# Three re-orderings in a two-layer image kernel: when a weight is loaded, when accumulators are seeded, when weight sums are made

## The chip, the cores and the metric

The kernel runs on one core of one Trainium2 chip. Its five engines work side by side, each through its own queue of instructions in order: PE (TensorE, matrix products; its weight loads are shown apart as PEld), DVE (VectorE), ACT (ScalarE), POOL (GpSimd) and SP (SyncE, which here only issues transfers). Sixteen DMA engines move data between the chip's memory, where the arrays lie, and the on-chip memory SBUF. PE writes into PSUM, eight banks from which DVE and ACT read. The metric is the device time of one execution in microseconds, the median over several runs.

## What is computed

Two layers over an image batch of 2 x 56 x 56 positions with 384 channels, in float32. The first layer is neighbourhood attention and an MLP. The second, around which the change lies, is this (cut to what matters):

```python
h = layernorm(x, n1_g, n1_b)
p = h @ w_in + b_in                                  # 384 -> 768
local = depthwise_conv_3x3(p, k_conv)
lr, rl = ema(local, axis=2), ema(local, axis=2, reverse=True)
tb, bt = ema(local, axis=1), ema(local, axis=1, reverse=True)
mixed = layernorm(0.25 * (lr + rl + tb + bt) + local, on_g, on_b)
x = x + (mixed @ w_out + b_out)                      # 768 -> 384
h2 = layernorm(x, n2_g, n2_b)
x = x + (gelu(h2 @ w1 + b1, approximate=False) @ w2 + b2)   # 384 -> 1536 -> 384
```

with `ema` the recurrence y[i] = 0.6 y[i-1] + 0.4 x[i].

## The kernel before

The 6272 positions are 49 tiles of 128 rows, taken in groups of four (one group has a single tile). The function `passes` holds everything after the attention.

The first pass goes over the groups of the first layer's MLP and, a group behind, the second layer's first normalisation and the product with `w_in` (`project_in`). Its result goes to the chip's memory (`p_d`).

The convolution and the four recurrences run on DVE and ACT beside PE's products. A small planner (`Beside`) holds a list of jobs: a `Band` loads some rows of one 128-channel slice (`pt`, L1280), multiplies by the centre tap on ACT (`loc`, L1295), adds the eight other taps on DVE (L1312), scans the lines both ways (`both`, L1258 and L1262), stores to `loc_d` and `mix_d` (L1320), and has POOL add `both` into `mix_d` (L1331). A `Columns` job does the vertical scans: loads (`loc`, L1350), turns (`line`, L1360), scans, turns back (`mixed`, L1378), and adds to `mix_d` through POOL. `beside.go(us)` is called after each block of PE's work and emits as many steps of these jobs as fit in the time given. This is a budget used when the program is written out; on the chip each engine follows its own order. The pool `conv` holds these tiles, with two buffers for loads, three for `loc` and `line`, four for `both` and `mixed`.

The second pass begins after the last `project_in`. Its weights `w1` and `w2` of the second layer come from `weights(1)` in three parts each (`w_parts`, 768 KB a part, L674, on SP's queue). The parts of `w1` are issued in the first pass's last group, the parts of `w2` right behind the last `project_in`.

The first three groups of the second pass (`dgroups[:switch]`, groups 0 to 2) run beside the convolution. A group does:
- twelve hidden blocks (m = 0 to 11): three matmuls of 128x512 (the profile shows each as two) into one of three PSUM banks `mm` (L1205), then gelu on ACT (L1216) into `hid`. Between them, statistics of the next group's `mixed` tokens: six transposing matmuls (`xi`, L1448), then DVE (L221, L222). Behind block 6, POOL turns these into a standard deviation `sd` and its inverse `rs` (L229, L230);
- `project_out` for the next group: six products with `w_out` (twelve matmuls as profiled) for each of four tiles. Tiles 0, 1 and 3 accumulate onto a bank, `y` or `y_end`, that ACT has seeded with the residual times `sd` (`seed_out`, L1487); ACT multiplies the result by `rs` (L1498). Tile 2 is evicted by DVE (L1508). The first two seeds of the group are written ahead, before the last hidden block;
- four products with `w2` (L1223, `y<-w,hid`), onto banks seeded by ACT (L1233), evicted by ACT (L2040).

From group 3 on (the tail), the two MLP products are made by a scheme of seven products in place of eight (`hidden_by_seven`, `tokens_by_seven`), which needs sums and differences of quarters of the weights and inputs: `w1_sums`, `xsums`, and four sums of `w2` (`sums_of_w2`, L1715, DVE). The sums of `w2` are needed in `tokens_by_seven`. In `hidden_by_seven`, three rounds u = 0, 1, 2 each make matmuls into `ua`, `uz` and `ub` (L1657); ACT copies `ub` out in between (L1690, L1696, L1703); DVE adds (`hid_u`: L1704, and L1676 within `finish`); gelu is L1664; POOL makes three sums of hidden blocks (L1721 to L1723). Twice in a round the loop calls `next(measuring)`, which emits one step of measuring the next group's tokens on DVE: a step is eight transposes of 32x192 (L1460); every second step also has statistics. Then `project_out` makes four tiles with DVE evicting each (L1508). Its hook `then(k)` issues, for k = 0, the last `finish`; before the change also one sum of `w2` per tile, in the first tail group alone; and the measuring of the fourth tile.

The tail's tiles come from a pool `tail` opened where `conv` has been closed, so its tiles lie over those of `conv`, one after the other in the order in which they are first asked for; an instruction that writes such a tile first waits for the last user of what lay there.

Of the kernel before, what the change touches and what calls it, by code (L numbers as in the profile page):

```python
# [45 lines left out]
HID, NHID = 4 * C, 4 * C // P  # L46
# [132 lines left out]
def block_kernel(ctx: ExitStack, tc: tile.TileContext, ins: dict, out: bass.AP):  # L179
    nc = tc.nc  # L180
# [187 lines left out]
    hT = ep.tile([P, NC, PAIR], F32, name="hT")  # L368
# [294 lines left out]
    def weights(layer):  # L663

        w1 = wm.tile([P, NC, HID], F32, name=f"w1_{layer}", tag="w1")
        w2 = wm.tile([P, NHID, C], F32, name=f"w2_{layer}", tag="w2")
        s1 = ins[f"L{layer}_conv_w1"].rearrange("(c p) n -> p c n", p=P)
        s2 = ins[f"L{layer}_conv_w2"].rearrange("(c p) n -> p c n", p=P)
        parts = []
        for h in range(0, HID, HID // 3):  # L670
            parts.append((w1[:, :, h : h + HID // 3], s1[:, :, h : h + HID // 3]))
        for c in range(0, NHID, NHID // 3):
            parts.append((w2[:, c : c + NHID // 3, :], s2[:, c : c + NHID // 3, :]))
        return w1, w2, [lambda q=nc.sync, d=d, s=s: q.dma_start(out=d, in_=s) for d, s in parts]  # L674
# [96 lines left out]
    for q in range(0, len(stream), CHUNKS):  # L771
        part = []
# [92 lines left out]
    for t in range(NS + 2):  # L865
        part = parts[t] if t < NS else []
# [16 lines left out]
        for s in fresh:  # L883
            if s % UG == 0:
                dense = Dense(s // UG)
            if s == NU - UG - 4:
# [3 lines left out]
                w1, w2, w_parts = weights(0)  # L890
# [211 lines left out]
    def passes(xs, xn, w1, w2, between=lambda ps: None):  # L1102
# [9 lines left out]
        switch = 3  # L1112
# [341 lines left out]
        def measure_by_vector(mx, norm, k):  # L1454


            t = tp.tile([P, NI * P], F32, name="turned", bufs=2)
            for i in range(0, P, HD):
                for j in range(0, P, HD):
                    nc.vector.transpose(  # L1460
                        t[j : j + HD].rearrange("p (m c) -> p m c", m=NI)[:, :, i : i + HD],
                        mx[i : i + HD, :, k * P + j : k * P + j + HD],
                    )
                if i == HD:
                    yield
            norm.add(k, [t[:, h * C : (h + 1) * C] for h in range(2)])
            yield
# [63 lines left out]
        sum_steps, seeds = [], []  # L1531
# [72 lines left out]
        def measure_by_steps(ahead, tiles):  # L1604
            for k in tiles:
                yield from measure_by_vector(ahead[0], ahead[2], k)
# [100 lines left out]
        def sums_of_w2(w2, engine=nc.gpsimd):  # L1707

            q = NHID // 2
            b11, b12 = w2[:, :q, : C // 2], w2[:, :q, C // 2 :]  # L1710
            b21, b22 = w2[:, q:, : C // 2], w2[:, q:, C // 2 :]
            t1, t2, t3, t4 = (tp.tile([P, q, C // 2], F32, name=f"w2_t{i}") for i in range(4))
            steps = []
            for to, x, y in ((t1, b12, b11), (t2, b22, t1), (t3, b22, b12), (t4, b21, t2)):
                steps.append(lambda to=to, x=x, y=y: engine.tensor_tensor(to, x, y, ALU.subtract))  # L1715
            return (t1, t2, t3, t4), steps
# [96 lines left out]
        w1_sums = more_of_w1(w1, sums_of_w1(w1, tp.tile([P, NC, HID // 2], F32, name="w1_t")))  # L1813
        x = xs.pop(0)
        hT = channels(xn, groups[0][1], "L0_conv_ln2_g", "L0_conv_ln2_b")
        add_row(x, groups[0][1], "b2_0")

        for g, (t0, n) in enumerate(groups):
# [19 lines left out]
            if g == last:  # L1838
                beside.until((0, NI - 1))
                load_row(0, "b2_1")  # L1840
                ahead = load_mix(0)
                beside.rate = 1.0
            if g < last:
                x_next, n_next = xs.pop(g + 1), groups[g + 1][1]
# [92 lines left out]
            if g == last:  # L1937
                ahead[2].close_both_ways(dgroups[0][1])
                w1, w2_1, w_parts = weights(1)
                for part in w_parts[:3]:  # L1940
                    part()
            if early:
                hT = io.tile([P, NC, MT], F32, name="hT")
            elif 0 < g < last:
                hT = channels(xn_next, n_next, *ln2)
            x2 = io.tile([P, NT, C], F32, name="xc")
            norm = Norm(sm)
            if early:
                for i, _ in enumerate(tokens_by_seven(low, high, *s12, w2, w2_sums, x, x2)):
                    if 0 <= i < n_next:  # L1950
                        turned(xn_next, i, hT)
                    if i == 5:
                        scaled(hT, n_next, *ln2)
                        xsums = sums_of_input(hT)
# [19 lines left out]
            if g == 0:  # L1974
                hT = channels(xn_next, n_next, *ln2)
                xsums = sums_of_input(hT)
                w2_sums, sum_steps = sums_of_w2(w2)
# [11 lines left out]
        g, x2, norm_w = waiting  # L1989
# [6 lines left out]
        hT = channels(xn, groups[g][1], *n1)  # L1996
# [6 lines left out]
        ahead = load_mix(1)  # L2003
        w2 = w2_1
        project_in(g, hT, first_input)
        for part in w_parts[3:]:
            part()
        n2 = "L1_conv_n2_g", "L1_conv_n2_b"

        hT = channels(first["xn"], dgroups[0][1], *n2)  # L2010
        add_row(x3, dgroups[0][1], "b2_1")
        for g, (t0, n) in enumerate(dgroups[:switch]):
            hid = []
            if g == 1:
                three = sums_of_w1(
                    w1, wp.tile([P, NC, INNER], F32, name="w1_t", tag="w_in")
                )
            for m in range(NHID):
                if m == NHID - 1:
                    seeds = [seed_out(*ahead[1:], k) for k in range(2)]  # L2020
                hid.append(hidden(w1, m, hT, n, "L1_conv_b1"))
                beside.go(MLP, measure_beside(m, g + 1, ahead))
            res = x3
            x3, norm, seeds = project_out(
                g + 1, *ahead, seeds=seeds, behind=lambda k: seeded(res, k)
            )
            ahead = load_mix(g + 2)
            for k in range(n):
                if k == n - 1:
                    hT = channels(xn, dgroups[g + 1][1], *n2)  # L2030
                ps = tokens(hid, w2, k, onto=seeds.pop(0))
                if k == 0:
                    norm.shift(dgroups[g + 1][1])
                if k == n - 3:
                    xn = normalized(norm, x3, dgroups[g + 1][1])
                beside.go(ROW)
                if k == n - 1:
                    add_row(x3, dgroups[g + 1][1], "b2_1")
                o = res[:, k, :]
                nc.scalar.copy(o, ps)  # L2040
                nc.sync.dma_start(out=yout[t0 + k * P : t0 + (k + 1) * P, :], in_=o)
                if k + 2 < n:
                    seeds.append(seeded(res, k + 2))
                if g == switch - 1 and k == 2:
                    beside.until((1, NI - 1))
                    cctx.close()
                    tp = pctx.enter_context(tc.tile_pool(name="tail", bufs=1, reuse_waits="tile"))
                    w1_sums = more_of_w1(w1, three, nc.vector)
# [2 lines left out]
        ps_y, ps_u, bank_b, banks_b = open_banks(pctx, "tail")  # L2051
        ps_m = ps_u
        xsums = sums_of_input(hT, nc.vector)
        w2_sums, sum_steps = sums_of_w2(w2, nc.vector)
        for g, (t0, n) in enumerate(dgroups):
            if g < switch:
                continue
            if g == dlast:
                hid = [hidden(w1, m, hT, n, "L1_conv_b1") for m in range(NHID)]
                for k in range(n):  # L2060
                    ps = tokens(hid, w2, k, y_end)
                nc.vector.tensor_copy(rows[:, 1, :], x3[:, n - 1, :])
                assert n == 1 and t0 + n * P == T2
                break
            n_next = dgroups[g + 1][1]
            add_row(ahead[1], n_next, "b_out")
            s1, s2 = (tp.tile([P, NHID // 2, MT // 2], F32, name=x) for x in ("s1", "s2"))
            low, high, finish = hidden_by_seven(
                hT, xsums, w1, w1_sums, (s1, s2), measure_by_steps(ahead, range(min(n_next, 3))),
                "L1_conv_b1",  # L2070
            )
            ahead[2].close(min(n_next, 3))
            more = measure_by_steps(ahead, range(3, n_next))

            def then(k):
                if k == 0:
                    finish()
                if sum_steps:
                    sum_steps.pop(0)()
                next(more, None)  # L2080
                if k == 1 and n_next > 3:
                    ahead[2].close(n_next, first=3)

            res = x3
            x3, norm = project_out(g + 1, *ahead, then)
            if g + 2 <= dlast:
                ahead = load_mix(g + 2)
            hT = io.tile([P, NC, MT], F32, name="hT")
            for i, _ in enumerate(tokens_by_seven(low, high, s1, s2, w2, w2_sums, res, res)):
                if i == 0:  # L2090
                    norm.shift(n_next)
                    xn = normalized(norm, x3, n_next)
                if 1 <= i <= n_next:
                    turned(xn, i - 1, hT)
                if i == 5:
                    scaled(hT, n_next, *n2)
                    xsums = sums_of_input(hT) if n_next == NT else None
                    add_row(x3, n_next, "b2_1")
            nc.sync.dma_start(
                out=yout[t0 : t0 + NT * P, :].rearrange("(k p) c -> p k c", p=P), in_=res  # L2100
            )
# [8 lines left out]
    with tc.If(again > 0):  # L2110
        attention_again()
        w1, w2, w_parts = weights(0)
# [81 lines left out]
```

## Time and profile before

| what | value |
|---|---|
| median of 3 runs | 2573.22 us (2570.5 to 2573.25) |
| profiled execution, own time | 2575.16 us |
| its span, first to last instruction | 2573.4 us |
| mean granted TensorE clock | 0.995 |
| last `project_in`, its p_d store issued | 1654.00 us |
| groups 0, 1, 2 of the second pass, first hidden matmul | 1654.69, 1743.36, 1827.58 us |
| tail, first matmul of `hidden_by_seven` | 1915.46 us |
| first and second `tokens_by_seven` | 1964.41, 2037.59 us |

Times in the trace count from the span's first instruction. A line of a timeline gives the start, the duration, the engine (PEld, and SPq for what SP issues), the line of the program, the operation, its output and inputs, how many instructions were merged, and in brackets the idle time before it with what ended it. A line of waits gives the engine and line that waited, what released it, and the total, the number and the longest. "Granted clock" is the share of full speed at which PE was allowed to run.

### The profile page before, as it was taken

The page shows a single profiled execution, that of the slowest core. Times are in us where ns is not written, and L with a number is a line of the kernel's source. Part 1 is how long each engine was busy: PE and PEld are TensorE (multiplying, and loading weights), DVE is VectorE, ACT ScalarE, POOL GpSimd, SP SyncE. Part 2 cuts the span into 40 slices and gives each one's busy share as a digit, 9 for nine tenths or more (in the row PEclk, how much of TensorE's full clock was granted, in tenths as well). Part 3 has the DMA queues.
Part 4 walks back from the last instruction along what each step waited for, and adds up shares of the span by engine and source line. Part 5 has one row for each costly group of instructions (what it writes and reads, how often), then busy time and mean ns, then how long its engine had stood idle before and what let it go on. Part 6 is the DMA issues. An engine that isn't in the chain of part 4 may idle for free. (4 is left out here: it accounts for less than half of the span.)

```text
span 2573.4 us, 41871 instructions
## 1 busy us (share of the span) xinstructions
PE 2535.8 (99%) x16678; PEld 1736.1 (67%) x16678; DVE 1982.8 (77%) x3706; ACT 1137.3 (44%) x2058; POOL 575.4 (22%) x618
## 2 busy tenths in 40 slices
PE   9999999999999999999999999999999999999999
PEld 5666666666698887455545555555468888888888
DVE  3888878887554453899989999789978877878871
ACT  5655555654443444334455443433862233233222
POOL 0111111111442331010110002112113333333332
PEclk9999999999999999999999999999999999999999
DMA  7423454225522223467677667766780333333210
GB/s 226 150 94 95 148 187 159 86 84 194 158 60 85 68 68 90 140 177 214 177 209 280 209 186 218 232 184 168 207 218 18 74 74 74 74 74 74 47 28 21
DMA packets 155597, 342.97 MB, mean 133 GB/s; under 512 B 11158, under 2 KB 112000, under 8 KB 153088
## 3 DMA queue, kind: packets, MB, share of 16 engines
q1 hardware_dynamic: 124096, 255.65, 29.4%
q0 software_dynamic: 26352, 57.81, 13.2%
q10 hardware_dynamic: 4944, 26.74, 3.0%
q8 instruction: 133, 2.18, 0.4%
q14 instruction: 72, 0.59, 0.1%
HBM read 176.39 MB, written 134.88 MB: 121 GB/s over the span
## 5 line engine op out<-in xcount | busy, mean ns | idle before, releaser
L1312 DVE SCALAR_TENSOR_TENSOR loc<-pt,taps,loc 128x495 f32<-128x495 f32 (+13 forms) x288 | 372.7, 1294 | 38.2 <-ACT loc L1295 29.5
L1205 PE MATMUL mm<-hT,w 128*128 128x512 f32 x720 | 318.9, 597 | 4.4 <-ACT hid L1216 4.2
L581 ACT ACTIVATE pts<-pts 119x448 f32<-119x448 f32 (+5 forms) x396 | 210.7, 573 | 109.4 <-DVE pts L571 100.3
L571 DVE TENSOR_TENSOR pts<-sc,bias 119x448 f32<-119x448 f32 (+5 forms) x396 | 219.2, 616 | 45.2 <-PE sc L560 44.9
L1205 PEld LDWEIGHTS mm<-hT,w 128*128 128x128 f32 x720 | 135.2, 191 | 166.4 <-issue 155.4
L1188 DVE STREAM_TRANSPOSE hT<-xn 32x96 f32<-32x96 f32 x784 | 211.2, 269 | 26.7 <-ACT xn L265 16.6
L414 PE MATMUL ps<-hT,wqkv 128*128 128x448 f32 x504 | 206.5, 554 | 2.1 <-ACT vs L459 1.5
L1460 DVE STREAM_TRANSPOSE turned<-mx 32x192 f32<-32x192 f32 x528 | 194.8, 369 | 10.2 <-DMA mix_d<-mixed 3.4
L1223 PE MATMUL y<-w,hid 128*128 128x384 f32 x552 | 181.9, 486 | 0.0
L1223 PE MATMUL y_end<-w,hid 128*128 128x384 f32 x552 | 181.8, 486 | 0.0
L1223 PEld LDWEIGHTS y_end<-w,hid 128*128 128x128 f32 x552 | 104.6, 190 | 72.1
L1223 PEld LDWEIGHTS y<-w,hid 128*128 128x128 f32 x552 | 104.3, 190 | 71.3 <-issue 0.5
L1216 ACT ACTIVATE hid<-mm,chan 128x512 f32<-128x512 f32 x120 | 82.1, 685 | 156.7 <-PE mm L1205 156.7
L414 PEld LDWEIGHTS ps<-hT,wqkv 128*128 128x128 f32 x504 | 91.9, 191 | 85.5 <-issue 75.4
L1205 PE MATMUL mm<-hT,w_in 128*128 128x512 f32 x324 | 140.8, 593 | 0.6 <-DVE hid_u L1676 0.6
L1331 POOL DMA_DIRECT2D mix_d<-both x36 | 31.8, 884 | 417.6 <-ACT both L1327 357.3
L1657 PE MATMUL ua<-hT,w 128*128 128x256 f32 x504 | 122.5, 379 | 0.0
L560 PEld LDWEIGHTS sc<-qT,kT 32*100 32x100 f32 (+3 forms) x3168 | 87.8, 169 | 46.8 <-DVE sum L590 7.6
L600 PE MATMUL o<-pts,vt 100*32 100x112 f32 (+3 forms) x3168 | 116.3, 263 | 0.9 <-ACT pts L581 0.9
L1205 PEld LDWEIGHTS mm<-hT,w_in 128*128 128x128 f32 x324 | 61.2, 190 | 77.5 <-issue 72.2
L1664 ACT ACTIVATE hid<-hid_u,chan 128x256 f32<-128x256 f32 x168 | 76.1, 500 | 82.0 <-DVE hid_u L1676 67.5
L237 POOL TENSOR_TENSOR rs<-rs,mhalf 128x4 f32<-128x4 f32 (+4 forms) x56 | 50.2, 897 | 277.2 <-DVE rs L234 276.1
(217 smaller groups left out, 5007.6 us busy)
## 6 DMA issues: line engine op xcount, KB each, us to landing
loc<-loc_d SPq DMA_DIRECT2D x24, 784.0 KB
xa<-x_d SPq DMA_DIRECT2D x24, 768.0 KB
xa<-rows POOLq DMA_DIRECT2D x24, 768.0 KB, 11.9
bias<-in_bias_t ACTq DMA_DIRECT2D x13, 1344.0 KB
p_d<-mx SPq DMA_DIRECT2D x11, 1536.0 KB
mx<-mix_d SPq DMA_DIRECT2D x11, 1536.0 KB
v_d<-vs SPq DMA_DIRECT2D x49, 192.0 KB
xr<-in_x SPq DMA_DIRECT2D x49, 192.0 KB
```

What stands on the lines that cost most here:

```text
L414: nc.tensor.matmul(ps, lhsT=wqkv[:, c, m * P : (m + 1) * P], rhs=hT[:, c, half_of(n)], start=c == 0, stop=c == NC - 1,)
L560: nc.tensor.matmul(sc[i // 2][: w.keys, i % 2, q : q + TT], lhsT=kT[d, hg, w.keys_at + r * w.kc : w.keys_at + (r + w.rows) * w.kc], rhs=qT ...
L571: nc.vector.tensor_tensor(self.pts[:n, h : h + 2, lo:hi, :], sc[half][:n, :, at * TT : (at + hi - lo) * TT].rearrange("p h (c q) -> p h c ...
L581: nc.scalar.activation(t, t, AF.Exp)
L600: nc.tensor.matmul(o[i * HD : (i + 1) * HD, self.slot, :TT], lhsT=w.vt[:n, c, h * HD : (h + 1) * HD], rhs=self.pts[:n, i, c, :], start=c = ...
L1188: nc.vector.transpose(hT[j : j + HD, :, k * P + i : k * P + i + HD], xn[i : i + HD, k, :].rearrange("p (c q) -> p c q", c=NC)[:, :, j : j ...
L1205: nc.tensor.matmul(ps[:, : n * P], lhsT=w[:, c, m * P : (m + 1) * P], rhs=hT[:, c, : n * P], start=c == 0, stop=c == NC - 1,)
L1216: nc.scalar.activation(t[:, : n * P], ps[:, : n * P], AF.Gelu, bias=col(b1, m))
L1223: nc.tensor.matmul(ps, lhsT=t[:, k * P : (k + 1) * P], rhs=w[:, m, :], start=m == 0 and onto is None, stop=m == len(lhs) - 1, skip_group_c ...
L1312: nc.vector.scalar_tensor_tensor(to, pt[:, lo + dy - self.top : hi + dy - self.top, xt : xt + n], self.tap(dy, dx), to, ALU.mult, ALU.add,)
L1460: nc.vector.transpose(t[j : j + HD].rearrange("p (m c) -> p m c", m=NI)[:, :, i : i + HD], mx[i : i + HD, :, k * P + j : k * P + j + HD],)
L1657: nc.tensor.matmul(bank[:, i, :], lhsT=w[:, m * P : (m + 1) * P], rhs=x, start=start and i == 0, stop=True, skip_group_check=True,)
```

## The change

Three edits in `passes`.

1. The three parts of `w2` (`w_parts[3:]`) are no longer issued right after the last `project_in`. They are issued in group 0 of the second pass, one each ahead of the hidden blocks m = 4, 6 and 8. In the program as built, SP's queue then has two loads of `pt`, one store to `loc_d` and one to `mix_d` ahead of the three parts, where they stood behind them; the three parts stay next to each other.
2. The first two seeds of `w_out`'s accumulators are written ahead of hidden block 10 in place of 11, in each of the three groups. On ACT the two L1487 move past one hidden gelu, in group 0 also past one `loc`, in group 2 also past four `mixed`.
3. The four sums of `w2` on DVE are made in the first tail group's `hidden_by_seven`, one behind each of the measuring steps 2 to 5 (counted from 0), in place of one behind each tile of `project_out`. Their tiles are asked for at step 2, so after `s1`, `s2`, `hid_u1`, `hid_u2` and `turned` and not before them; the tail pool's layout changes with it.

The number of instructions on each engine is the same.

```diff
@@ second pass, ahead of its groups @@
         project_in(g, hT, first_input)
-        for part in w_parts[3:]:
-            part()
         n2 = "L1_conv_n2_g", "L1_conv_n2_b"
@@ groups 0 to 2 @@
             for m in range(NHID):
-                if m == NHID - 1:
+                if g == 0 and m in (4, 6, 8):
+                    w_parts.pop(3)()
+                if m == NHID - 2:
                     seeds = [seed_out(*ahead[1:], k) for k in range(2)]
                 hid.append(hidden(w1, m, hT, n, "L1_conv_b1"))
                 beside.go(MLP, measure_beside(m, g + 1, ahead))
@@ tail @@
         xsums = sums_of_input(hT, nc.vector)
-        w2_sums, sum_steps = sums_of_w2(w2, nc.vector)
+        w2_sums = None
+
+        def with_sums(steps):
+
+            nonlocal w2_sums
+            for i, _ in enumerate(steps):
+                if w2_sums is None and i == 2:
+                    w2_sums, sum_steps = sums_of_w2(w2, nc.vector)
+                if i >= 2 and sum_steps:
+                    sum_steps.pop(0)()
+                yield
+
...
+            steps = measure_by_steps(ahead, range(min(n_next, 3)))
             low, high, finish = hidden_by_seven(
-                hT, xsums, w1, w1_sums, (s1, s2), measure_by_steps(ahead, range(min(n_next, 3))),
+                hT, xsums, w1, w1_sums, (s1, s2), with_sums(steps) if g == switch else steps,
                 "L1_conv_b1",
             )
...
                 if k == 0:
                     finish()
-                if sum_steps:
-                    sum_steps.pop(0)()
                 next(more, None)
```

## The prediction, made before the changed kernel was run

> **What bounds the kernel now.** I read the engines' busy times first, then TensorE's waits, then the timelines around each wait that the change can touch. The first line of the page settles the kind of answer:
>
> ```profile
> PE 2535.8 (99%) x16678; PEld 1736.1 (67%) x16678; DVE 1982.8 (77%) x3706; ACT 1137.3 (44%) x2058; POOL 575.4 (22%) x618
> ```
>
> TensorE (PE) carries the span. The change neither adds nor removes a matmul, so it can only change PE's gaps and the half-speed matmuls behind some of them. PE's waits from 1650 us to the end are five (total, times, longest):
>
> ```profile
> PE mm L1205 <- ACT hid L1216: 4.2, 1, 4.2
> PE y_end L1223 <- ACT y_end L1487: 4.0, 1, 4.0
> PE xi L1448 <- DVE st L221: 2.7, 1, 2.7
> PE y L1749 <- DVE xc L1508: 2.3, 1, 2.3
> PE ub L1657 <- issue: 2.2, 1, 2.2
> ```
>
> PE's timeline gives place and after-effect (start, duration, group, gap before it):
>
> ```profile
> 1669.64 2.74 PE L1205 MATMUL mm<-hT,w 128*128 128x512 f32 x6
> 1676.63 5.49 PE L1205 MATMUL mm<-hT,w 128*128 128x512 f32 x6 [4.25 <-ACT hid L1216]
> ...
> 1865.31 5.83 PE L1223 MATMUL y_end<-w_out,mx 128*128 128x384 f32 x12 [4.04 <-ACT y_end L1487]
> ...
> 1922.27 1.10 PE L1657 MATMUL ub<-xsums,w_t 128*128 128x256 f32 x4 [2.19 <-issue]
> ...
> 1964.41 5.85 PE L1749 MATMUL y<-w,hid 128*128 128x192 f32 x24 [2.25 <-DVE xc L1508]
> ```
>
> Behind three gaps the same matmuls take longer: six take 5.49 instead of 2.74 (and the next transposes 0.92 instead of 0.82), twelve 5.83 instead of 4.03, twenty-four 5.85 instead of 4.06. In half-microsecond windows the granted clock stands at 0.50 there (1675.5 to 1682, 1866.5 to 1869.5, 1965.5 to 1968.5). So the gaps cost 4.25+2.75+0.10 = 7.1, 4.04+1.80 = 5.84, 2.25+1.79 = 4.04 and 2.19 us. The gap before xi (2.72 us, at 1754.95) has no slow matmuls behind it.
>
> **Part 1, w2 later: 7.1 us.** Why ACT was late at 1676 is in its timeline, and SP's tells why the load was:
>
> ```profile
> 1663.38 0.69 ACT L1216 ACTIVATE hid<-mm,chan 128x512 f32<-128x512 f32 x1 [1.89 <-PE mm L1205]
> 1674.78 1.23 ACT L1295 ACTIVATE loc<-pt,taps 128x1120 f32<-128x1120 f32 x1 [10.71 <-DMA pt<-p_d]
> ...
> 1654.00 0.37 SPq L1546 DMA_DIRECT2D p_d<-mx  x1
> 1654.47 5.77 SPq L674 DMA_DIRECT2D w<-in_L_conv_w  x3
> 1663.86 2.19 SPq L1280 DMA_DIRECT2D pt<-p_d  x2
> ```
>
> The band's centre tap L1295 sits fourth in ACT's queue, ahead of the fourth hidden block, and waits for its pt load. That load goes out behind three pieces of w2 (3 x 768 KB) on SP's queue. ACT stands still 10.7 us, PE's three mm banks fill, PE stops at 1672.4. Afterwards the three issues (5.77 us of SP) stand behind pt x2, loc_d and mix_d. What follows them on SP is a pt load at 1689.40, far behind. The reader of w2 (y<-w,hid) starts at 1711.09; the stretch's DMA traffic, the same bytes, has ended by 1681.5 (DMA share 1.0 before, 0.03 after), so about 30 us cover it, and only w2 landing later than that would cost PE, one for one.
>
> pt may not go before p_d is stored: released by 1663.9 as now, or sooner with w2 out of the way. Its landing alone is not shown. Nearest rows are POOL's accumulating stores on another queue: 756 to 784 KB in 6.7 to 10.4 us, 532 KB in 8.1 us, for 588 KB here. At best it lands before ACT asks (1664.1); at worst 8 us after 1663.9, at 1671.9. L1295 (1.23) and one hid (0.69) then end at 1673.8, a 1.4 us gap, so the part is worth 5.7 to 7.1. I take 7.1, as landing by 1670.5 is enough and w2 is no longer ahead. DVE gains up to the 9.82 us that it idled before 1676.04, but the next band's centre (L1295 at 1693.75) stands behind a hid that PE paces, so from there it moves with PE. The xi gap stays.
>
> **Part 2, seeds one hidden block earlier: 5.84 us, less 0.2.** In the third group ACT runs hid, four `mixed`, hid, four `mixed` (the second half held 0.52 us by a DMA), two seeds, hid:
>
> ```profile
> 1861.05 1.66 ACT L1378 ACTIVATE mixed<-line 128x392 f32<-128x392 f32 x2
> 1863.23 1.65 ACT L1378 ACTIVATE mixed<-line 128x392 f32<-128x392 f32 x2 [0.52 <-DMA mix_d<-mixed]
> 1864.68 0.58 ACT L1487 ACTIVATE y_end<-xa,sd 128x384 f32<-128x384 f32 x1
> ```
>
> Moved ahead of hid 10, the seeds stand behind the first four `mixed`, which end at 1860.75. The first is done at 1861.33, when PE's last hidden matmul ends (1861.27): no gap. Hid 10 comes 1.1 us later; its bank has no later user in the loop. The second four `mixed` now delay hid 11 and the first eviction to 1866.2, 0.9 us after PE is done, so ACT and DVE gain some 5.0 where PE gains 5.84. The last seed of this group is written at 1906.46 for a PE that wants it at 1907.12, 0.66 of slack, so about 0.2 comes back. In groups 0 and 1 PE does not wait for the seeds: nothing. They need `sd` from POOL (L230), ready at 1689.4 and 1772.4 against a hid 9 ending at 1691.3 and 1775.6.
>
> **Part 3, w2's sums.** Removed: two L1715 (2.41 and 1.33) ahead of the third w_out eviction. DVE reaches it at 1963.75, 3.74 earlier without them, and y would be free at 1960.6, before PE wants it at 1962.15. All 4.04 us go.
>
> A side effect: the tail pool hands out memory in the order of first request. In the built programs hid_u1's first buffer lies at byte 142240 before, inside the last `mixed` tile (139360 to 145632), whose store DVE's and ACT's first tail instructions then await:
>
> ```profile
> 1921.58 0.59 ACT L1696 COPY hid_u<-ub 128x512 f32<-128x512 f32 x1 [4.43 <-DMA mix_d<-mixed]
> ```
>
> After, it lies at 123808, in a `line` tile that ACT has finished by 1910.55; the sums' own tiles take the `mixed` places, and are written some 5 us after that store has landed. So the 2.19 gap at 1922 goes.
>
> Added: the four sums between measuring steps. In one round of the loop DVE has two eight-block transposes (3.06 each), statistics (1.2), L1676 (0.69) and L1704 (0.64), 8.7 us in PE's 9.5; it idles 0.92 before each L1676. Then ACT needs 1.4 (a gelu pair, L1696) before PE's next ub matmuls, with 0.3 to spare (1931.54 against 1931.84). Before the first L1676 one sum of 1.33 is added: 1.33-0.92-0.30 = 0.1 late. Before the second, three: 3.99-1.84-0.30-0.1 = 1.75 late. The second sum overlaps POOL's last sum of hidden (L1723); together such a pair took 2.41 and 2.38 instead of 1.33 and 1.27, so some 0.25 more. New gaps: 2.1 us in all (bounds: 1.85 uncontended; 3 x 2.41 less the slack and one half-speed stretch of 1.8, 6.9). The fourth sum delays L1704 and the first eviction by about 1.3, absorbed by DVE's 1.96 idle before the third L1676.
>
> Whether the new gap halves the clock: the row at 1964 (2.25 us) says 1.79 more, the rows at 1922 (2.19) and 1754 (2.72) say nothing more; I take nothing, two rows of three. The Trainium skill (TensorE: Matmul & The Clock Gate, section "Why this matters for your kernels") allows idle gaps up to about 3 us before the clock halves; by it the removed gap at 1964 would be worth 2.25, not 4.04, and the sum 1.8 less. The trace disagrees there (0.50 after 2.25 us), and decides.
>
> **Sum.** 7.1+5.84-0.2+4.04+2.19-2.1 = 16.9 us. The profiled execution took 2575.16 for a span of 2573.4; the runs' median is 2573.22. From the median: 2556.3.
>
> **Rivals.**
> 1. *The sums on PE's path cost more* (all beside POOL, and a half-speed stretch): -6.9 instead of -2.1, gain 12.1, 2561.1. For it: POOL's sums of hidden fill 3.9 of each 9.5 us there. Against: only the second and fourth are beside them. 0.13.
> 2. *p_d, not w2, holds pt*: it lands as late as now, part 1 is void, gain 9.8, 2563.4. For: SP waited 3.6 us for p_d even after issuing w2. Against: w2 no longer stands between. 0.07.
> 3. *DVE runs ahead and the xi gap goes too*: 2.7 more, 2553.6. Against: the wait on L1295 at 1693.75. 0.08.
> 4. *DVE is the real pace* (busy about 220 of 254 us from 1654 to 1908) and PE's gains return as waits for statistics: under 5 us stay, about 2570. Against: its largest idles, 9.82 and 6.19, are these same stalls. 0.05.
> 5. *Slower: seeds wait for `sd`.* ACT runs in order; if POOL's L230 comes late, hid 10 and every hid behind it stand still, PE fills its banks, three groups over. The margins are 1.9, 3.2 and over 7 us. It decides once sd is later than hid 9 by over 5.6 us plus the bank slack in each group; at 6 us each plus a half-speed 1.8 it costs 23, about 2580. POOL's pow took 2.0 beside DVE and 1.0 without, too little. 0.03.
>
> **How the numbers follow.** The forecast has 0.64: own range 2553.5 to 2560 (part 1 at 5.7, the seeds' return at 1, one half-speed stretch). The whole range runs from everything going at once (2551.5) to rival 2 (2564). A measurement of this kernel can tell 0.2% (5.1 us) from no change. Faster by more: forecast and rivals 1 to 3, 0.92; same, 0.05; slower, 0.03.
>
> **What would show it.** Right: L1295 near 1664 to 1670 without a long DMA wait; no clock under 1 near 1676 and 1866; `y_end` without a wait for L1487; L1696 without a wait for `mix_d`; a new wait of ub in the first tail group behind ACT's L1696, 1.5 to 2.5 us, ahead of it L1676 late by a sum; the y matmuls of L1749 without a wait for L1508. Wrong: a pt wait that remains, or a gap elsewhere in 1690 to 1915 where none was.

## The result and the profile after

The changed kernel takes 2556.97 us (median of four runs, 2553.55 to 2561.95) against 2572.48 for the kernel before in the same comparison: a ratio of 0.9942, 95% interval 0.9924 to 0.996. That is 15.5 us less; 2556.3 was predicted.

The profiled execution of the changed kernel took 2561.95 us, its span is 2560.1 us (2573.4 before) and its mean granted TensorE clock 0.996. The page's row of busy times (us, share of the span, instructions; two matmul records are missing from this trace):

```profile
PE 2532.6 (99%) x16676; PEld 1734.6 (68%) x16678; DVE 1983.6 (77%) x3706; ACT 1138.0 (44%) x2058; POOL 577.5 (23%) x618
```

PE's waits from 1640 us to the end (us in total, times, longest us) were five and are three:

```profile
PE xi L1448 <- DVE st L221: 2.7, 1, 2.7
PE ub L1657 <- ACT hid_u L1696: 1.8, 1, 1.8
PE y_end L1223 <- ACT y_end L1233: 0.4, 1, 0.4
```

The waits for the late hid (4.2), for the seeds (4.0), for `mix_d` at ub (2.2, shown as issue) and for L1508 (2.3) are gone. The one at xi has stayed, and two are new. PE's timeline at these places (start, duration, group, gap before it):

```profile
1749.42 0.90 PE L1448 MATMUL xi<-ident,mx 128*128 128x128 f32 x3 [2.72 <-DVE st L221]
1750.12 6.59 PE L1205 MATMUL mm<-hT,w 128*128 128x512 f32 x12
...
1857.24 4.14 PE L1223 MATMUL y_end<-w_out,mx 128*128 128x384 f32 x12
...
1897.94 8.01 PE L1223 MATMUL y_end<-w,hid 128*128 128x384 f32 x24 [0.43 <-ACT y_end L1233]
...
1932.22 1.13 PE L1657 MATMUL ub<-xsums,w_t 128*128 128x256 f32 x4 [1.77 <-ACT hid_u L1696]
```

Twelve mm matmuls behind xi take 6.59 us here, where the same twelve take 5.32 at full clock (1671.39 in this trace): the gap at xi now has a half-speed stretch behind it. Twelve w_out matmuls take 4.14 right at the seeds, against 5.83 before.

SP and ACT in group 0 (SPq rows are SP's issues):

```profile
1655.74 0.37 SPq L1546 DMA_DIRECT2D p_d<-mx  x1
1665.15 0.81 SPq L1280 DMA_DIRECT2D pt<-p_d  x2
...
1667.19 3.49 SPq L674 DMA_DIRECT2D w<-in_L_conv_w  x3
1669.67 1.23 ACT L1295 ACTIVATE loc<-pt,taps 128x1120 f32<-128x1120 f32 x1 [3.85 <-DMA pt<-p_d]
```

With w2 behind it pt lands 4.5 us after its issue (1665.15 to 1669.67). Before it took 10.9 (1663.86 to 1674.78). The store p_d that has to end first took 9.4 us, against 9.9 with w2's three pieces queued behind it.

DVE and ACT in the first tail group:

```profile
1928.80 1.36 DVE L1715 TENSOR_TENSOR w_t<-w 128x1152 f32<-128x1152 f32 x1
1930.08 0.68 DVE L1676 TENSOR_TENSOR hid_u<-uz,hid_u 128x512 f32<-128x512 f32 x1
...
1930.80 0.91 ACT L1664 ACTIVATE hid<-hid_u,chan 128x256 f32<-128x256 f32 x2 [3.32 <-DVE hid_u L1676]
1931.61 0.56 ACT L1696 COPY hid_u<-ub 128x512 f32<-128x512 f32 x1
```

This is the new wait of ub as the prediction drew it: a sum stands ahead of L1676, two gelus wait for L1676, and the copy that frees ub's bank comes behind them.

**Where the 13 us between the two spans came from.** I cut the second half at PE's first hidden matmul of conv groups 0, 1 and 2 and at the first ua matmul of the tail's first and second group. That gives stretches A, B, C and D (A: group 0; B: group 1; C: group 2; D: the tail's first group). Everything behind D takes 579.8 to 579.9 us in thirteen of the fourteen profiles of this study (580.3 in the first of the two with the sums on GpSimd), and the piece from the first ua matmul of the first pass (near 690 us) to A takes 961.8 to 961.9. So a span differs from another only in A to D and in the first 690 us, which no edit here touches.

| profile | first 690 | A | B | C | D |
|---|---|---|---|---|---|
| before | 692.9 | 88.67 | 84.22 | 87.88 | 78.03 |
| after | 694.6 | 81.39 | 85.80 | 82.75 | 73.91 |
| after less before | +1.7 | -7.28 | +1.58 | -5.13 | -4.12 |

The five add up to -13.2, the difference of the two spans. The three parts are in A, C and D; the +1.58 and the +1.7 are half-speed clock and the start of the kernel, taken up below.

### The profile page after: what moved, and what is told of

Same layout as the page of the kernel before. It is cut to its first block, busy times and chain, and to the rows that moved or that the text cites. A ratio compares the mean times of both kernels' runs of the same rounds, so it can differ in the third digit from the quotient of the medians.

```text
span 2560.1 us, 41867 instructions
## 1 busy us (share of the span) xinstructions
PE 2532.6 (99%) x16676; PEld 1734.6 (68%) x16678; DVE 1983.6 (77%) x3706; ACT 1138.0 (44%) x2058; POOL 577.5 (23%) x618
## 3 DMA queue, kind: packets, MB, share of 16 engines
q0 software_dynamic: 26352, 57.81, 13.2%
## 5 line engine op out<-in xcount | busy, mean ns | idle before, releaser
L237 POOL TENSOR_TENSOR rs<-rs,mhalf 128x4 f32<-128x4 f32 (+4 forms) x56 | 50.3, 898 | 271.9 <-DVE rs L234 270.8
```

## The experiments

All are compared with the kernel before, run beside them on the same chip; its median there was 2573.58, 2573.19 and 2572.41 in three comparisons, with single runs from 2567 to 2579. Stretches come from one profiled execution each.

**Each part alone: w2's pieces.**

```diff
-        for part in w_parts[3:]:
-            part()
...
+                if g == 0 and m in (4, 6, 8):
+                    w_parts.pop(3)()
```

> Before with part 1 alone (w2's three pieces behind the two pt loads). Theory of the prediction: the 4.25 us gap of PE in the first group of the second pass and the half-speed matmuls behind it go, nothing else moves: from the group's first hidden matmul to the next group's 88.67 us become 81.4 to 81.7, the later stretches (84.22, 87.88 and 78.03 us in before) stay as they are but for half-speed stretches of 1.7 us each; the median is 7 us lower, 2565.5. Rival (p_d's store, not w2, holds the pt load): ACT still waits some 10 us at the centre tap, the gap of 4.25 stays, median unchanged. Rival (DVE is the pace): the stretch shrinks, but 3 us or more return as new waits of PE in the next two groups.

Measured: A 81.45, B 85.60, C 87.75, D 77.90; median 2567.22, ratio 0.998 (0.9969 to 0.9991). The stall in group 0 goes with this edit alone, while C and D keep theirs; both rivals (p_d's store, DVE's pace) fall. B is 1.4 above the 84.22 of the kernel before, the half-speed stretch behind xi. The median is 1.7 us above the expected 2565.5.

**The seeds alone.**

```diff
-                if m == NHID - 1:
+                if m == NHID - 2:
                     seeds = [seed_out(*ahead[1:], k) for k in range(2)]
```

> Before with part 2 alone (seeds ahead of hidden block 10). Theory: the third group's stretch, 87.88 us in before, becomes 82.2 to 82.8 (the wait for the seed and the half-speed matmuls, 5.84, less 0.2 to 0.7 that returns at the last seed of the group); the first two groups' stretches stay (88.67, 84.22); median 5.1 to 5.6 us lower, 2567. Rival (ACT only shifts the wait: the second half of the mixed copies now delays the first eviction): PE waits 1 us or more at a later w_out or w2 product, and the stretch is over 84. Rival (seeds wait for sd): a wait of PE for a hidden block in one of the three groups.

Measured: C 82.31, as expected, but a median of 2572.6 where 2567 was expected, ratio 0.9996 (0.9987 to 1.0005): no gain that can be told. Its profile shows one part of the loss in the tail. ACT's copy that waits for `mix_d`, and PE behind it:

```profile
1919.79 0.58 ACT L1696 COPY hid_u<-ub 128x512 f32<-128x512 f32 x1 [4.94 <-DMA mix_d<-mixed]
1920.47 1.11 PE L1657 MATMUL ub<-xsums,w_t 128*128 128x256 f32 x4 [2.70 <-issue]
1921.41 1.88 PE L1657 MATMUL ub<-hT,w 128*128 128x256 f32 x4
```

PE reaches the tail earlier and the store's landing has not moved by as much: ACT waits 4.94 instead of 4.43, PE 2.70 instead of 2.19, and four matmuls behind it take 1.88 instead of 1.03, at half clock. So part of what the seeds save is lost again in a wait that the third part of the change takes away.

**The sums alone, and the sums with their tiles where they were.** The first is the third part of the change, whole. The second moves the sums but asks for their tiles first, as before; these are its lines.

```diff
+            for i, _ in enumerate(steps):
+                if i >= 2 and sum_steps:
+                    sum_steps.pop(0)()
+                yield
...
-                if sum_steps:
-                    sum_steps.pop(0)()
```

> Before with part 3 alone (sums of w2 behind measuring steps, tiles asked for late). Theory: from the first tail group's first matmul to the second's 78.03 us become 73.7 to 74.2: the gaps at ub (2.19) and at the first product of tokens_by_seven (2.25 and 1.79 at half speed) go, a new gap of 1.7 to 2.1 us comes at ub in the third round behind ACT's L1696; median 4 us lower, 2568.5. Rival (the ub gap has nothing to do with memory): the 2.19 gap stays and the stretch is 76. Rival (sums dear): gap of over 3 us or half speed behind it, stretch over 75.5.

> Before with the sums behind the measuring steps as in part 3, but the sums' tiles asked for first as in before, so that hid_u1 lies in the last mixed tile again. Theory: ACT's L1696 waits some 4.4 us for the mix_d store again and PE's gap of 2.2 us at ub is back, the wait for L1508 stays away: stretch of the first tail group 75.8 to 76.4 (73.9 and the 2.2 back). Rival (memory does not matter): the same stretch as with part 3 alone, 73.7 to 74.2, and no wait for mix_d.

Measured: D 73.39 with the whole part (median 2569.14, ratio 0.998, 0.9971 to 0.9989) and 75.76 with the old layout (2570.46, 0.9987, 0.9976 to 0.9999). The first is 0.3 us under the expected band, as the new gap at ub is 1.47 where 1.7 to 2.1 was expected. ACT and PE with the old layout:

```profile
1921.18 0.58 ACT L1696 COPY hid_u<-ub 128x512 f32<-128x512 f32 x1 [4.48 <-DMA mix_d<-mixed]
1921.86 1.10 PE L1657 MATMUL ub<-xsums,w_t 128*128 128x256 f32 x4 [2.23 <-issue]
```

PE's gap in front of the tail's second ub group is back, and ACT's L1696 waits 4.48 us for `mix_d`, against 1.29 for PE with the new layout. That the layout is worth 2.4 us is shown from this side, and from the other by the next run.

**The layout alone.**

```diff
-        w2_sums, sum_steps = sums_of_w2(w2, nc.vector)
+        w2_sums, sum_steps = None, []
...
+                if w2_sums is None:
+                    w2_sums, sum_steps = sums_of_w2(w2, nc.vector)
```

> The kernel before, with the tiles of w2's sums asked for after the first of hid's tiles, and the sums where they stood, behind tiles of the tail's product. Theory (the 2.19 in front of ub is the address of hid_u1 over the last mixed tile, whose store has to land; the 2.25 at L1749 is the sums' place): the gap of 2.19 goes and the 2.25 stays, the tail's first group takes 75.5 to 76 us (78.03 before). Rival (the layout does nothing by itself): 77.5 to 78. For the clock: a gap is followed by a half-speed stretch of 3.41 us or a multiple where 2.0 to 2.1 us or more of it lie within one window of a grid of 3.413 us steps, on which all half-speed stretches of a run begin, and not where 1.9 or less do.

Measured (one run): D 75.55 against 78.0, the 2.19 gone and 2.26 at L1749 still there; ACT's L1696 waits 1.29 us, for PE. The rule on the clock was right for every gap of this run and of the three others that ran with it (below).

**Two pieces of w2 ahead of pt instead of three.**

```diff
+        for _ in range(2):
+            w_parts.pop(3)()
...
-                if g == 0 and m in (4, 6, 8):
+                if g == 0 and m == 4:
                     w_parts.pop(3)()
```

> The changed kernel, with two of w2's three pieces issued ahead of the loads of pt again and only the third at m=4. Theory (pt's packets come after those of whatever stands ahead of them on SP's queue, some 2.1 us a piece: the landing came 4.5 us after its issue with none ahead and 10.8 with three): ACT's wait for pt is some 8 us (3.85 with none), TensorE's gap in front of mm returns at 1 to 2 us of the 4.25, and the stretch from group 0's first hidden matmul to group 1's is 83 to 84 us (81.4 with none ahead, 86.4 to 88.7 with three). Rival (any store of weights ahead delays pt as much as three): gap of about 4 us, stretch of 86 to 88.5. Second rival (only the third piece matters): no gap, 81.4.

SP and ACT in this run:

```profile
1651.49 2.69 SPq L674 DMA_DIRECT2D w<-in_L_conv_w  x2
1660.80 1.87 SPq L1280 DMA_DIRECT2D pt<-p_d  x2
...
1669.01 1.23 ACT L1295 ACTIVATE loc<-pt,taps 128x1120 f32<-128x1120 f32 x1 [7.92 <-DMA pt<-p_d]
```

ACT waits 7.92, PE's gap at mm is 1.46, and A takes 84.28, just over the 83 to 84 expected (one run). pt lands 8.2 us after its issue with two pieces ahead, 10.9 with three and 4.5 with none, some 2 us for each 768 KB ahead of it. The rivals (any piece delays it as much; only the third counts) fall.

**The change without the seeds, and the change again.** The edit of the first, to the changed kernel:

```diff
-                if m == NHID - 2:
+                if m == NHID - 1:
```

> The changed kernel without its second part: w_out's seeds stand where they stood. Theory (the seeds take a gap of some 4 us with a half-speed stretch behind it from the path, whatever the other two parts do): the stretch from group 2's first hidden matmul to the tail's first is back at 87 to 88.5 us (82.75 with the seeds ahead), the stretch before it stays at 81.4 and the tail's first group at 73.4 to 74; the median is 4.5 to 6 us above that of the whole change. Rival (the seeds alone took only 1.0 us off the median, so they are worth about that): the median is 0.5 to 1.5 us above the whole change.

> The whole change once more, for its interval beside the others: 2553.5 to 2558 us, 14 to 18 below the kernel before.

Measured: without the seeds A 81.44, B 84.22, C 87.79, D 73.36, median 2561.65, ratio 0.9957 (0.9944 to 0.997). The change again: C 82.65, D 74.17, median 2560.19, ratio 0.9952 (0.994 to 0.9965), 2 us above the expected band. The stretch C came back as expected. The medians differ by 1.5 only, where 4.5 to 6 was expected and the rival said 0.5 to 1.5; against the result above, taken in another comparison, it is 4.7. The intervals overlap, so the medians decide nothing here. Of the 5.1 in C, D returns 0.8 (0.33 of it at ub, whose gap is 1.44 without the seeds and 1.77 with them) and B 1.5, the half-speed stretch behind xi that the profile without the seeds happened not to have.

**The seeds alone, again.**

> The seeds alone, once more. Its stretch from group 2's first hidden matmul to the tail's shrank by 5.6 us and its median only by 1.0. Theory (chance of the clock: the first 690 us, where the code is that of the kernel before, took 3.9 us longer in the profiled run, and gaps of 2 to 3 us have a half-speed stretch behind them or not by their place on a grid of 3.41 us that runs on from before the kernel starts): the stretch takes 82 to 82.8 us again, the first 690 us are as long as in other runs (688 to 697), and the median is 2 to 5 us below the kernel before's. Rival (the earlier seeds cost elsewhere what they save): the median is again within 1 us of the kernel before, and the first 690 us or the tail are again longer by 3 us or more.

Measured: C 83.33, first 690 us 690.0, D 80.18 (ub's gap 2.63 with half-speed matmuls behind it), median 2569.94, 2.5 below the kernel before, ratio 0.9995 (0.9984 to 1.0005). The long first 690 us of the earlier profile (696.7) were chance, as the theory had it. A longer tail is there again, by 2.2 us where the rival had 3 or more. What the seeds save in C they lose in D by 0.5 and 2.2 us in the two profiles when part 3 is missing. By the stretches a gain of some 4 us is left: A to D take 333.2 and 336.6 in these two profiles, and 339.0 without any part of the change (the means over all profiles with the old code in a stretch, 87.2, 85.6 and 88.2, and for D 78.0, over the two that have neither the seeds nor the sums moved). The two medians show 1.0 and 2.5, and a gain of 4 lies outside the interval of the first.

The span and granted clock of every run, profiled or not, say where to look. The span times (1 - clock), the time lost to half speed, averages 13.1 and 11.8 us in the two comparisons, against 11.5 and 11.3 for the kernel before beside them; the rest of the span is 2.6 and 1.9 us shorter. So PE does wait less, but the time at half speed, which should have fallen with the seeds' gap, did not fall by these means (uncertain by about 1 us each). A likely place is ub: its gap is 2.04 to 2.23 us in the profiles with the old layout and the old seeds (none of three has half speed behind it) and 2.63 to 2.70 with the new seeds (both have). That this is all of it is not shown, as only profiled runs show their stretches.

**All four sums on GpSimd, behind the load of xa's rows.**

```diff
-                if w2_sums is None and i == 2:
-                    w2_sums, sum_steps = sums_of_w2(w2, nc.vector)
-                if i >= 2 and sum_steps:
-                    sum_steps.pop(0)()
+                if w2_sums is None:
+                    w2_sums, sum_steps = sums_of_w2(w2)
+                    for step in sum_steps:
+                        step()
```

> The changed kernel with all four sums of w2 on GpSimd, started at measuring step 0, so that no sum stands between the two L1676 of the tail's measuring and the L1696 copies that ub waits for. Theory (the ub gap of 1.77 is the price of DVE's two sums ahead of L1676): the gap in front of ub is gone or under 0.3 us, the first tail group takes 72 to 72.3 us instead of 73.9, no new wait appears, since GpSimd ends its four sums some 10 us before ub's product needs them, and the median falls by 1.5 to 2 us. Rival (the sums come too late on GpSimd, each 2.4 to 2.7 us): PE waits for xsums at L1657, the tail's first group takes 75 us or more. Second rival (ub's gap is ACT's own row of work, not the sums): gap of 1.5 to 2 us stays.

The gap of 1.77 at ub is gone, so it was DVE's sums. But D is 73.18, not 72 to 72.3, and the median 2559.67 (ratio 0.995, 0.9937 to 0.9963), no better. DVE and GpSimd in this run:

```profile
1927.78 2.70 POOL L1715 TENSOR_TENSOR w_t<-w,w_t 128x1152 f32<-128x1152 f32 x1
1930.41 1.30 POOL L1721 TENSOR_TENSOR s<-hid 128x512 f32<-128x512 f32 x1
...
1938.03 0.87 POOL L237 TENSOR_TENSOR rs<-rs,mhalf 128x3 f32<-128x3 f32 x1
1938.94 0.62 DVE L1508 SCALAR_TENSOR_TENSOR xc<-y,rs,xa 128x384 f32<-128x384 f32 x1 [7.21 <-POOL rs L237]
```

L237, a tiny operation that the evictions need, stands behind 19 us of GpSimd's sums, back to back from 1919.27 on. DVE idles 7.21 us for it, its evictions come late, and PE waits 1.50 for L1508 at L1749. Expecting "no new wait" was wrong: it went by when the sums end, not by what queues behind them.

**The measuring beside group 1 at odd blocks.**

```diff
-            k = (m - 1) // 2 - 2 if g == 0 else m // 2
+            odd = 1 if g in (0, 2) else 0
+            k = (m - odd) // 2 - (2 if g == 0 else 0)
...
-            if m % 2 == (1 if g == 0 else 0) and 0 <= k < n:
+            if m % 2 == odd and 0 <= k < n:
...
-            if m == 6 and g:
+            if m == 6 + odd and g:
```

> The changed kernel, with the measuring beside the hidden blocks of group 1 moved from even blocks m to odd ones, so that it no longer stands on DVE behind the work of the conv at the block where xi's transposes wait for L221. Theory (the gap of 2.72 at xi, which the change leaves, is this order on DVE): the gap goes or falls under 0.5 us and with it the half-speed stretch that stood behind it in seven profiles of nine; the stretch from group 1's first hidden matmul to group 2's goes from 85.8 to 81.5 to 82.5 us; the median falls by 3 to 4.3 us below the change's. Rival (measuring an eighth later leaves sd late for the seeds two blocks from the end): a gap in front of y_end of 1 to 2 us appears instead, and the stretch stays over 84 us. Second rival (xi is late because of its own vector chain, not of measuring): the 2.72 stays.

Measured: xi's gap 1.43 (0.5 at most was expected), no half-speed stretch behind it, B 82.93 (81.5 to 82.5 was expected), and no new wait of PE elsewhere (ACT waits 1.5 for L230 at a seed, the beginning of the first rival). Median 2554.61, ratio 0.9932 (0.9918 to 0.9946). PE at xi:

```profile
1742.82 0.55 PE L1448 MATMUL xi<-ident,mx 128*128 128x128 f32 x3 [1.43 <-DVE st L221]
1743.20 5.32 PE L1205 MATMUL mm<-hT,w 128*128 128x512 f32 x12
```

The order on DVE is thus half of that gap, and what is left of it lies below the point at which the clock falls. This is the lowest median of the study, 4.2 us under the median of the change's nine runs (2558.83, from two other comparisons) and 3.3 us by the stretches; the intervals overlap.

**Odd blocks, and the sums on GpSimd ahead of the load.** The last run's edit, with the four sums issued before `add_row(ahead[1], n_next, "b_out")`, and the tiles `s1`, `s2` and `hid_u2` asked for later so that none lies over a late `mixed` tile.

```diff
+            if w2_sums is None:
+                w2_sums, sum_steps = sums_of_w2(w2)
+                for step in sum_steps:
+                    step()
             add_row(ahead[1], n_next, "b_out")
```

> The change with the measuring at odd blocks as in the run with that alone, and with all four sums of w2 on GpSimd ahead of the load of xa's rows, in GpSimd's idle stretch behind the last group's stores, their tiles over memory that is free by then. Theory (in the run with the sums on GpSimd behind that load, GpSimd's L237 for the tokens waited 7 us behind them and gave a gap of 1.50 at L1749; ahead of it they end before the sums of hid begin): no gap over 0.5 us in the first tail group, which takes 71.8 to 72.4 us; with xi's gap gone too, 4 to 6 us under the change's median, 2551 to 2553. Rival (the sums wait for the memory or slow DVE's pair): the first tail group takes 73.5 us or more. Second rival (the odd blocks cost as much as they save): median as the change's.

Measured: D 82.68 where 71.8 to 72.4 was expected, median 2563.63, ratio 0.9965 (0.9952 to 0.9978), worse than the change. DVE and GpSimd at the tail's start (the edit moves the line numbers by one to three: L1639 here is L1638 of the changed kernel, L1718 is L1715, L1705 is L1704):

```profile
1897.12 3.83 DVE L1639 TENSOR_TENSOR xsums<-hT 128x256 f32<-128x256 f32 x1 [3.02 <-ACT hT L282]
1900.98 2.76 DVE L1639 TENSOR_TENSOR xsums<-xsums,hT 128x256 f32<-128x256 f32 x1
1903.66 2.92 DVE L1639 TENSOR_TENSOR xsums<-hT 128x256 f32<-128x256 f32 x1
1906.50 2.89 DVE L1639 TENSOR_TENSOR xsums<-hT,xsums 128x256 f32<-128x256 f32 x1
...
1897.45 3.20 POOL L1718 TENSOR_TENSOR w_t<-w 128x1152 f32<-128x1152 f32 x1
1900.73 2.72 POOL L1718 TENSOR_TENSOR w_t<-w,w_t 128x1152 f32<-128x1152 f32 x1
1903.42 2.87 POOL L1718 TENSOR_TENSOR w_t<-w 128x1152 f32<-128x1152 f32 x1
1906.26 2.85 POOL L1718 TENSOR_TENSOR w_t<-w,w_t 128x1152 f32<-128x1152 f32 x1
```

Four xsums that take 0.42 us each in the changed kernel take 2.76 to 3.83, each ending 0.3 us behind the GpSimd sum that it ran beside. DVE is 10 us late, and PE waits 0.5 and 1.7 for xsums and 5.3 for L1705, with two half-speed windows at its end and behind it. The rival that the sums slow DVE decided.

## Why the prediction was right

**Part 1 (7.1).** A fell by 7.28. pt's load landed 4.5 us after its issue, inside the bounds (landing at 1664.1 to 1671.9), and p_d released it 9.4 us after its own issue, "as now or sooner". But 7.1 is what this profile of the kernel before had. In five other profiles with w2's pieces in their old place A is 86.37 to 87.36, the gap 3.2 to 4.1 with one window of half clock, not two. Over the six the mean is 87.2, and the part is worth 5.8. The term was sized from the longest of six stalls.

**Part 2 (5.84 less 0.2).** C fell by 5.13. PE waits 0.43 for the last group's late seed instead of 0.2; the 0.3 that is then still missing from 5.84 is in no gap of 0.1 us or more. Over all profiles C is 88.2 with the seeds in the old place (six of them) and 82.9 with them moved (eight): 5.4. The prediction missed that this depends on part 3: with `hid_u1` still over the `mixed` tile the wait for `mix_d` takes part of it back. In the change as a whole that wait is gone. What the seeds are worth is shown by the stretches alone: no pair of medians tells 5 us from 1.

**Part 3 (4.04 and 2.19 less 2.1).** D fell by 4.12; 4.13 was the sum. Both old gaps went, the layout by itself is worth about what was said (2.4 for 2.19), and the new gap is 1.77 where 2.1 was put, without half-speed matmuls behind it. Its cause is shown by the run with the sums on GpSimd, where it is gone. That the sum fits to 0.01 is luck, since 1.77 in place of 2.1 should have left 4.46. No half speed behind the new gap was taken from two rows of three; by the rows of the last section a gap of 1.77 is too short for it, and one of 2.1 is on the edge.

**The gap at xi.** It stayed at 2.72, so rival 3 fell; the run with odd blocks shows that the order of the measuring on DVE makes 1.3 of it. "No slow matmuls behind it" was one draw: ten of twelve profiles with this gap have a half-speed stretch behind it, and 84.22 for B was the exception. That is the +1.58, no effect of the change.

**The sum.** With the mean of the profiles for each part it is 5.8 + 5.4 + 4.0 (D is 73.6 to 74.2, mean 74.0, in the four kernels with all three parts, and 78.0 without them) = 15.2, against 16.9 predicted and medians of 15.5 and 13.0 in two comparisons. So the forecast overstated the gain by 1.7, most of it the dear draw at mm. That it still came within 0.7 us of the first median is luck: the five later runs of the same kernel have 2560.19, 3.9 above the forecast and just above the stated 2553.5 to 2560.

**The rivals.** 1 (dearer sums): 1.77, not 6.9. 2 (p_d holds pt): pt landed 6.4 us sooner after its issue. 4 (DVE is the pace): A, C and D kept their gains. 5 (seeds wait for `sd`): no wait of ACT for L230 in any profile of the change. With the measuring at odd blocks ACT did wait 1.5 us for it, and PE did not.

## What to carry to other kernels

Cut the trace at a few fixed instructions and compare stretches. Pieces without a long gap of PE repeat to 0.1 us here, and a piece with a gap near 2 us or more moves by 1.5 or more with the clock though its code is the same (B takes 84.2 or 85.6 to 85.9), so several profiles are needed for its mean. Stretches show where a gain of 5 us is made that the medians of five or six runs don't show; that the median gains as much is another question, as the seeds alone show. When work is moved to an idle engine, ask what small operation now queues behind it and which engine's two-input operations it will hold up, not only whether it ends in time. The address that a pool gives a tile is a dependency like any other: here the order of two requests was worth 2.4 us.

## What the runs showed of the hardware

**Half-speed stretches begin on a fixed grid.** In the 14 profiles there are 57 half-speed stretches ahead of each run's last 15 us. All last 3.4 us or twice that, and within a run all begin on one grid of 3.4133 us to within 0.02 us, from 26 us to 1965 us. The Trainium skill (TensorE: Matmul & The Clock Gate, section "Part 1: The HAM clock gate (the "warmup" mystery)") gives a free-running window of 3413 ns; the traces agree. What starts a half-speed window is the idle time within one window before it. The changed kernel's windows around xi (us, PE busy, granted clock, DMA share, GB/s):

```profile
1745.83:1749.24 3.41, 0.87 (x5) 1.00 1.02 281
1749.24:1752.66 3.42, 3.24 (x6) 0.50 1.08 313
1752.66:1756.07 3.41, 3.41 (x9) 1.00 0.53 123
```

The same gap of 2.72 us in the change without the seeds:

```profile
1742.83:1746.24 3.41, 1.78 (x7) 1.00 0.82 210
1746.24:1749.66 3.42, 2.33 (x8) 1.00 1.10 310
1749.66:1753.07 3.41, 3.41 (x10) 1.00 0.81 206
```

There the grid splits it, 1.63 and 1.09 us idle, and the clock stays at 1.00. Over the 49 gaps of 1 us or more from 1640 us on, a window with 2.13 us or more of the gap in it is always followed by half speed, and one with 1.91 or less never, unless it is at half speed already: such a window keeps it with 0.90 us or more (five cases) and leaves it with 0.58 or less (ten). The rule was put down after ten profiles and held for the 14 gaps of the four that came later. Each window at half speed costs PE some 1.7 us, half its length. So, with 2.02 us as the middle of 1.91 and 2.13, a gap of under 1.9 us costs itself, one of 2.72 costs a window more in about (3.41 + 2.72 - 2 x 2.02) / 3.41 = 0.6 of its possible places on the grid (an estimate; it was ten of twelve profiles), and one of 4 costs one window and sometimes two. The rule of the Trainium skill that the prediction weighed, gaps of up to about 3 us, is too kind by these rows.

**A GpSimd sum holds DVE's whole operation.** The xsums rows above show 0.42 us becoming 2.8 beside each GpSimd sum, while L1676, one of whose inputs is in PSUM, keeps its 0.69 beside one (at 1925.78 in the run with the sums on GpSimd). The Trainium skill (SBUF — State Buffer, section "SBUF: two separate sides") has a GpSimd operation and a DVE operation with two SBUF inputs lock a shared port pair for a whole instruction, while the other waits; these rows agree.

**The first 690 us vary.** They take 686.7 to 696.7 us over the 14 profiles, with the same code, which is more than any part of the change is worth.
